# Moving the tables of the last 16 heads into an idle activation block, and giving the residuals two buffers and GpSimd's queue

## The chip, the cores and the metric

The kernel runs on one core of a Trainium2 chip. A core has a matrix engine (PE; its weight loads are shown apart as PEld), a vector engine (DVE), a scalar engine (ACT), GpSimd (POOL) and a sync engine (SP) that here only issues DMAs. Each engine works through its own instructions in order and waits on semaphores for the others. The metric is device time in microseconds (us) of one execution, the median of several. A second kind of number comes from one profiled execution: its span, the busy time of each engine and the waits between instructions.

## The reference

The input `x` is 32 sequences x 64 channels (heads) x 1024 positions. Each head gets a state space convolution, each sequence is masked to its length, and then the last axis of 1024 goes through a gated feed-forward layer whose weights are 4 bit (GPTQ). The residual is added at the end. Cut to what matters:

```python
# convolution, per head h: kernel of length 1024 from 64 complex modes
dtA = (-exp(log_A_real) + 1j * A_imag) * exp(log_dt)[:, None]
K = 2 * einsum('hn,hnl->hl', Cc * (exp(dtA) - 1) / A, exp(dtA[:, :, None] * arange(1024))).real
u = x * mask                                   # mask: position < length of the sequence
y = (causal_convolution(u, K) + u * D) * mask  # written with an FFT of length 2048
# feed-forward, 1024 -> 2752 -> 1024, weights w = (q - z - 1) * s, s per group of 128 rows
gate, up = y @ Wg, y @ Wu
inter = gate * sigmoid(gate) * up
out = x + (inter @ Wd).astype(float16)
```

## The kernel before

The 64 heads x 32 sequences are 2048 columns, in four blocks of 512 columns (16 heads each). Positions and hidden units lie on the 128 partitions.

**The convolution of a block.** The kernel values of 8 heads come from tables. `decays` (L475) makes exponentials, `tables` (L443, calling `phase_tables`, L183) makes sines and squares, `factors` (L460, calling `kernel_factors`, L213) combines them on DVE into `e1t` and `e2t`. `make_kernel` (L421) multiplies these on PE (L425, L427), splits the product into two halves of 16 bit (L430 on ACT, L431 on DVE) and writes them to a DRAM buffer `kpad` (L433). `toeplitz` (L514) loads for one head a 512 KB matrix `t` from `kpad`, each row one place further on (L525, SP's queue). There are three `t` buffers. `conv_load` (L500) loads the input `u` of four heads. `conv_head` (L531) does one head: eight steps of three small matmuls each (L548). After every second head DVE masks the sum into `y` (L560), ACT rounds it to 16 bit `xh` (L563), and POOL computes the remainder `xl` (L565). The pair `xh`, `xl` of a block is kept in an activation buffer. There are two of them, `x[0]` for blocks 0 and 2 and `x[1]` for blocks 1 and 3, each 128 x 8 x 512 twice.

**The feed-forward.** A chain is one PSUM tile (128 x 2 x 512) that is multiplied up over groups of 128 rows and scaled between the groups, because every group has its own scale. `gu_one` and `gu_pair` (L678) do gate and up, 8 groups per chain; `dn_pair` (L718) does the down product for 256 of the 1024 outputs, 21 groups and a remainder (L736, L737, L741). After each group the PSUM tile is rescaled in place, by DVE (L637, `rescale_two`) or by two ACT instructions (L640), and PE's next group of that chain waits for this. Three or four chains are in flight, so PE works on the others meanwhile. At the end of a `dn_pair` chain the sum is scaled into `o` (L754 on DVE or L758 on ACT), the residual `xr` (512 KB, `residual`, L772) is added by POOL for one half and by DVE for the other (L762), and two stores of 256 KB go out (L767). `o` and `xr` have two buffers each.

**Stages.** `roll` (L780) runs eight stages: 0 and 1 gate and up of the blocks 0 and 1 for four column tiles, 2 the rest of gate and up for both, 3 the four down chains of block 0, 4 those of block 1, 5 gate and up of blocks 2 and 3, 6 and 7 their down chains. Beside the chains it advances side generators, listed in `sides` (L1040) with a rate: so many steps of the generator for each step of a chain. With `None` as the last entry the generator is advanced only if the planner's own clock has room on DVE and ACT (`room`, L327), and dropped at the stage's end; with `True` it is run to its end when the stage ends, with nothing between its steps. The order in which instructions stand on each engine comes from this plan and from a scheduler beneath it that may move an instruction whose inputs are known ahead of others.

**Around the change.** In stages 3 and 4 the convolutions of blocks 2 and 3 run beside the down chains (`convs`, L1024, 1.9 steps for each chain step). Block 3 needs the kernels of heads 48 to 63, which `fourth` (L1003) makes in two groups of eight. `fourth` first waits until all down weights are unpacked, closes the pool of the unpacking (`up_stack`) and opens a pool `kg2` in its room. It uses `x[1]` as scratch for the phase tables and the decays, since `x[1]` is free from the end of stage 2 until block 3's first heads are written. `convs` runs block 2, then forces all of `fourth`, then runs block 3. The residuals of blocks 0 to 2 are loaded by SP's queue into buffers that they share with `sg`, the output of the gate's activation (tag `sg`, two buffers), and so stand between SP's loads of `t` and `u`.

Of the kernel before, what the change touches and what calls it, by code (L numbers as in the profile page):

```python
# [9 lines left out]
F32 = mybir.dt.float32  # L10
# [19 lines left out]
KSCALE = 64.0  # L30
PLACES = {("a", "pair"): 1, ("a", "single"): 2, ("b", "pair"): 3}
MAGIC = 12582912.0
RATES = {"first": (0.5, 4.6), "fill": (1.0, 0.8), "third": 0.5, "convs": 1.9}
HOP, MM, LANDING = 220.0, 215.7, 6000.0
LAG, HEAD_STARTS = 2, [4, 2, 1]
DVE_ROOM, ACT_ROOM = 1200.0, 1500.0
# [211 lines left out]
def every(gen):  # L248
    for _ in gen:
        pass  # L250
# [8 lines left out]
class Core:  # L259
    def __init__(self, ctx, tc, io):  # L260
        self.tc, self.nc, self.io = tc, tc.nc, io
        pool = lambda name, **k: ctx.enter_context(tc.tile_pool(name=name, **k))
# [11 lines left out]
        self.forced = True  # L274
        self.bank_free = {"a": [], "b": []}
        self.kpad = self.dram.tile([H, 2, 1152], F16, name="kpad")
        self.dm, self.known, self.ready = {}, set(), set()
        self.marks = {}
        self.sg, self.t0, self.us, self.raw = {}, {}, {}, {}
# [438 lines left out]
    def dn_pair(self, k, blk, place):  # L718
# [8 lines left out]
        for g in range(GI):  # L727
# [14 lines left out]
            if g < 21:  # L742
# [4 lines left out]
                    nc.scalar.dma_start(self.ihl[:, g], self.spill[g])  # L747
                    self.loaded[blk + 1, g] = True
                yield
        xr = self.res[k] if blk == 3 else self.residual(self.fw, 2 * k, blk)  # L750
        take = self.last_o if blk == 3 else lambda shape, dt: self.fw.tile(shape, dt, name="o", bufs=2)
        o = take([128, 2, 512], F16)
        if not apart and self.on_dve(1240, 1380):
# [17 lines left out]

    def residual(self, pool, n0, blk):  # L772
        rows, cols = slice(128 * n0, 128 * n0 + 256), slice(512 * blk, 512 * blk + 512)
        xr = pool([128, 2, 512], F32) if callable(pool) else pool.tile([128, 2, 512], F32, name="xr", tag="sg", bufs=2)
        self.nc.sync.dma_start(
            xr, self.io["xT"].rearrange("l h b -> l (h b)")[rows, cols].rearrange("(k p) t -> p k t", p=128))
        return xr

# [64 lines left out]
def tile_ssm_ffn(ctx, tc, io):  # L843
    nc = tc.nc
    c = Core(ctx, tc, io)
# [141 lines left out]
    third_it = third()  # L987
# [13 lines left out]
        return make  # L1001

    def fourth():  # L1003
        c.forced = True
        every(third_it)
        c.forced = False
        while not c.ready.issuperset(("dn", k, part) for k in range(4) for part in range(3)):
            yield
        c.up_stack.close()
        with tc.tile_pool(name="kg2", bufs=1, side="right") as kg2:  # L1010
            space = c.x[1]
            yield from c.decays(c.scratch(space[:1]), (48, 56))
            c.taps(kg2, 48)
            for h0 in (48, 56):
                yield from c.tables(ScratchPool(c.scratch(space[1:])), h0, 8)
                yield from c.factors(kg2, h0, 8, c.xds[h0])
                for _ in range(3):
                    yield
                c.make_kernel(kg2, h0, 8, "a")
                yield  # L1020

    fourth_it = fourth()

    def convs():  # L1024
        yield from c.conv(2)
        c.forced = True
        c.need(*(("dn", k, part) for k in range(4) for part in range(3)))
        every(fourth_it)
        c.forced = False
        yield from c.conv(3)  # L1030

    def residuals():
# [3 lines left out]
        yield  # L1036

    convs_it = convs()
    second_it = second()
    sides = {  # L1040
        0: [(unpack_it, RATES["first"][0], None), (group_it, 1.0, None), (second_it, RATES["first"][1], True)],
        1: [(unpack_it, RATES["fill"][0], None), (third_it, RATES["fill"][1], None)],
        2: [(third_it, RATES["third"], None), (unpack_it, RATES["fill"][0], None)],
        3: [(unpack_it, RATES["fill"][0], None), (fourth_it, RATES["fill"][1], None), (convs_it, RATES["convs"], False)],
        4: [(fourth_it, RATES["fill"][1], None), (convs_it, RATES["convs"], True)],
        6: [(residuals(), 1.0, True)],
# [80 lines left out]
```

## Time and profile before

| | |
|---|---|
| time, median of 3 runs | 1074.12 us (1073.29 to 1074.46) |
| the profiled execution's own time | 1075.33 us |
| its span, first to last instruction | 1073.5 us |
| PE busy | 1026.2 us, 96% |
| DVE busy | 803.7 us, 75% |
| ACT busy | 775.6 us, 72% |
| POOL busy | 246.5 us, 23% |
| mean granted PE clock | 0.992 |

The page of the profile gives busy time by engine, the span in 40 slices, the DMA queues, the chain of work that ended last, the costliest groups of instructions, and the DMAs with the time from issue to landing. Queries give the same for a stretch of time: busy time by engine and granted clock (stretches), the instructions in order (timeline), who waited for whom (waits). A matmul's shown time, 0.38 us for 512 columns, includes the length of the pipeline; back to back such matmuls start 0.2157 us apart, so a busy PE may still have lost a little at each restart. Times below are counted from the span's start. Stages 3 and 4 lie at about 404 to 585 us.

### The profile page before, as it was taken

To read this page: it belongs to the slowest core of one execution; us is meant where nothing else is said; L and a number is where in the kernel's file an instruction comes from. 1 tells how busy PE (TensorE), PEld (TensorE's weight loads), DVE (VectorE), ACT (ScalarE), POOL (GpSimd) and SP (SyncE) were. 2 spreads that over 40 slices of the span, in tenths; PEclk is the share of its full clock that TensorE was granted. 3 is DMA by queue.
4 is the path that set the end of the run, shared out by engine and by line. 5 is a ranking of instruction groups with operands and counts; after the bars stand their busy time and mean duration, and the time that the engine had idled before them with its cause. 6 is when DMAs were issued, how large, how long until landed. Compare 5 with 4: busy or idle time off the path is not lost.

```text
span 1073.5 us, 15382 instructions
## 1 busy us (share of the span) xinstructions
PE 1026.2 (96%) x5854; PEld 513.5 (48%) x5854; DVE 803.7 (75%) x939; ACT 775.6 (72%) x1034; POOL 246.5 (23%) x270
## 2 busy tenths in 40 slices
PE   3989999999999999997999999999999999999996
PEld 2867444444344445663665444444444444444442
DVE  8965788888977786768446777777877777777776
ACT  5767777787677777777577777666666667878775
POOL 0333233232332242231103112221111222102102
PEclk9999999999999999999999999999999999999998
DMA  6976321111111534546753001000000001424102
GB/s 197 331 244 211 101 69 40 40 59 40 42 48 50 143 88 156 164 156 196 231 167 128 30 29 51 20 13 17 20 20 20 20 20 58 129 79 148 59 1 79
DMA packets 52099, 99.76 MB, mean 93 GB/s; under 512 B 9524, under 2 KB 11444, under 8 KB 52024
## 3 DMA queue, kind: packets, MB, share of 16 engines
q1 hardware_dynamic: 38888, 70.09, 20.8%
q0 software_dynamic: 5280, 17.31, 4.3%
q10 hardware_dynamic: 7856, 11.37, 3.6%
q8 instruction: 46, 0.75, 0.3%
q14 instruction: 29, 0.24, 0.1%
HBM read 78.99 MB, written 19.76 MB: 92 GB/s over the span
## 4 chain that ended last, share of the span: by engine, by line
PE 83%; ACT 5%; DMA 4%; DVE 4%; issue 2%; POOL 0%; SPq 0%; DVEq 0%; ACTq 0%
PE chq L687 23%; PE chq L688 22%; PE chq L736 13%; PE chq L737 13%; PE cq L548 6%; PE chq L664 2%; PE chq L665 2%; DMA t<-kpad 2%; ACT chq L640 1%; DVE chq L618 1%; ACT chq L620 1%; DVE v L700 1%; DMA ihl<-kpad 1%; DMA ihl<-xF 1%; PE chq L741 1%
## 5 line engine op out<-in xcount | busy, mean ns | idle before, releaser
L687 PE MATMUL chq<-xh,w 128*128 128x512 f16 x1216 | 460.4, 380 | 5.7 <-DVE chq L618 2.1
L688 PE MATMUL chq<-xl,w 128*128 128x512 f16 x1216 | 458.6, 380 | 0.0
L618 DVE TENSOR_SCALAR chq<-chq,gur 128x1024 f32<-128x1024 f32 x261 | 333.2, 1289 | 95.3 <-PE chq L688 94.1
L620 ACT ACTIVATE chq<-chq,gur 128x1024 f32<-128x1024 f32 x285 | 304.3, 1085 | 86.8 <-PE chq L688 85.5
L640 ACT ACTIVATE chq<-chq,dnr 128x512 f32<-128x512 f32 x372 | 242.1, 661 | 71.7 <-PE chq L737 63.8
L736 PE MATMUL chq<-ihl,wd 128*128 128x512 f16 x672 | 253.8, 380 | 6.5 <-ACT chq L640 3.5
L737 PE MATMUL chq<-ihl,wd 128*128 128x512 f16 x672 | 253.4, 380 | 0.0
L637 DVE TENSOR_TENSOR chq<-chq,dnr 128x1024 f32<-128x1024 f32 x129 | 158.4, 1231 | 83.6 <-PE chq L737 83.2
L688 PEld LDWEIGHTS <-w 128*128 128x128 fp8e4 x1216 | 118.9, 98 | 155.3 <-issue 19.4
L687 PEld LDWEIGHTS <-w 128*128 128x128 fp8e4 x1216 | 118.9, 98 | 145.9 <-issue 1.9
L310 POOL TENSOR_TENSOR ihl<-v,ihl 128x512 f16<-128x512 f32 x42 | 48.3, 1150 | 362.9 <-ACT ihl L629 362.9
L737 PEld LDWEIGHTS <-wd 128*128 128x128 fp8e4 x672 | 65.5, 98 | 76.0 <-issue 12.7
L548 PEld LDWEIGHTS <-t 128*128 128x128 f16 x1152 | 81.4, 98 | 39.2 <-DMA t<-kpad 5.9
L736 PEld LDWEIGHTS <-wd 128*128 128x128 fp8e4 x672 | 65.7, 98 | 67.7 <-issue 1.7
L548 PE MATMUL cq<-uh,t 128*128 128x256 f16 (+3 forms) x720 | 91.8, 226 | 4.6 <-DMA t<-kpad 4.5
L565 POOL TENSOR_TENSOR xl<-y,xh 128x512 f16<-128x512 f32 x28 | 36.2, 1294 | 161.5 <-ACT xh L563 161.5
L548 PE MATMUL cq<-ul,t 128*128 128x256 f16 (+3 forms) x360 | 71.6, 225 | 0.0
L629 ACT CAST ihl<-v 128x512 f16<-128x512 f32 x42 | 25.9, 617 | 58.7 <-DVE v L700 55.3
L700 DVE SCALAR_TENSOR_TENSOR v<-chq,gul,sg 128x1024 f32<-128x1024 f32 x38 | 48.6, 1280 | 17.1 <-PE chq L688 11.3
L310 POOL TENSOR_TENSOR spill<-v,spill 128x512 f16<-128x512 f32 x42 | 48.8, 1161 | 14.2 <-ACT spill L629 13.9
L640 ACT ACTIVATE chq<-chq,gur 128x512 f32<-128x512 f32 x66 | 43.2, 661 | 11.0 <-PE chq L665 9.8
L590 POOL TENSOR_TENSOR w<-w,z 128x256 int32<-128x256 int32 x42 | 31.5, 770 | 82.0 <-DVE w L584 77.6
(250 smaller groups left out, 820.5 us busy)
## 6 DMA issues: line engine op xcount, KB each, us to landing
t<-kpad SPq DMA_DIRECT2D x48, 512.0 KB, 4.4
spill<-spill POOLq DMA_DIRECT2D x42, 256.0 KB, 2.7
ihl<-spill ACTq DMA_DIRECT2D x42, 256.0 KB, 2.8
z<-zc SPq DMA_DIRECT2D x29, 256.0 KB, 3.7
u<-xF SPq DMA_DIRECT2D x12, 512.0 KB, 3.7
xr<-xT SPq DMA_DIRECT2D x12, 512.0 KB, 4.7
out<-xr POOLq DMA_DIRECT2D x24, 256.0 KB, 2.9
w<-qgu SPq DMA_DIRECT2D x21, 256.0 KB, 4.1
```

Source lines behind the costliest of these rows:

```text
L310: self.nc.gpsimd.tensor_tensor(out, a, b, op)
L548: nc.tensor.matmul(q[:, d:, h % 2, :], t0[:, lw, 128 * d:128 * d + 128], uu[:, 0:8 - d, h % 4, :], start=(d == 0 and k == 0 and h % 2 == 0 ...
L565: split.tensor_tensor(xl[:, :, ts], yv, xh[:, :, ts], ALU.subtract)
L618: self.mark("dve", self.nc.vector.tensor_scalar(q, q, col, None, ALU.mult))
L620: self.mark("act", self.nc.scalar.activation(q, q, AF.Copy, scale=col))
L637: self.mark("dve", self.nc.vector.tensor_tensor(q, q, cols.to_broadcast([128, 2, 512]), ALU.mult))
L640: self.mark("act", self.nc.scalar.activation(q[:, k], q[:, k], AF.Copy, scale=cols[:, k]))
L687: nc.tensor.matmul(q[:, b], lw, xh[:, g, :], start=(g == 0), stop=False, skip_group_check=True)
L688: nc.tensor.matmul(q[:, b], lw, xl[:, g, :], start=False, stop=(g == GH - 1), skip_group_check=True)
L700: nc.vector.scalar_tensor_tensor(v, q, last, self.sg.pop(ct - 21), ALU.mult, ALU.mult)
L736: nc.tensor.matmul(qs[j], lw, self.ihl[:, g, 0], start=(g == 0), stop=False, skip_group_check=True)
L737: nc.tensor.matmul(qs[j], lw, self.ihl[:, g, 1], start=False, stop=False, skip_group_check=True)
```

## The change

Three things change.

The residuals of blocks 0 to 2 no longer share buffers with `sg`. At the end of the first down chain the kernel makes sure that all down weights are unpacked, closes the pool of the unpacking, and opens a pool `xrp` of two buffers in its room. These residuals are loaded by GpSimd's queue, which also carries their stores. The residuals of block 3 stay with SP.

`fourth` takes all its room from `x[1]`: decays, the D coefficients, phase tables, factors and the split kernel. It waits neither for the unpacking nor for the third group of tables, so its steps can begin with stage 3. The three fixed pauses before `make_kernel` become a wait on the planner's clock.

`convs` doesn't force `fourth` after block 2; it idles until heads 56 to 63 are known, and forces only at the stage's end. Its rate goes from 1.9 to 1.52 steps for each chain step.

```diff
-RATES = {"first": (0.5, 4.6), "fill": (1.0, 0.8), "third": 0.5, "convs": 1.9}
+RATES = {"first": (0.5, 4.6), "fill": (1.0, 0.8), "third": 0.5, "convs": 1.52}
...
+        self.xrp = None
...
-        xr = self.res[k] if blk == 3 else self.residual(self.fw, 2 * k, blk)
+        if blk == 3:
+            xr = self.res[k]
+        else:
+            if self.xrp is None:
+                self.need(*(("dn", j, part) for j in range(4) for part in range(3)))
+                self.up_stack.close()
+                self.xrp = self.up_stack.enter_context(self.tc.tile_pool(name="xrp", bufs=2, side="right"))
+            xr = self.residual(self.xrp, 2 * k, blk)
...
-        xr = pool([128, 2, 512], F32) if callable(pool) else pool.tile([128, 2, 512], F32, name="xr", tag="sg", bufs=2)
-        self.nc.sync.dma_start(
+        xr = pool([128, 2, 512], F32) if callable(pool) else pool.tile([128, 2, 512], F32, name="xr")
+        (self.nc.sync if callable(pool) else self.nc.gpsimd).dma_start(
...
     def fourth():
-        c.forced = True
-        every(third_it)
-        c.forced = False
-        while not c.ready.issuperset(("dn", k, part) for k in range(4) for part in range(3)):
+        first, second = c.x[1]
+        yield from c.decays(c.scratch([first[:, :4]]), (48, 56))
+        c.taps(ScratchPool(c.scratch([first[:, 4:6]])), 48)
+        for h0 in (48, 56):
+            small = ScratchPool(c.scratch([first[:, 6:8], second[:, 7:8]]))
+            yield from c.tables(ScratchPool(c.scratch([second[:, :7]])), h0, 8)
+            yield from c.factors(small, h0, 8, c.xds[h0])
+            yield from c.pause(c.td - c.tp + HOP)
+            c.make_kernel(small, h0, 8, "a")
             yield
-        c.up_stack.close()
-        with tc.tile_pool(name="kg2", bufs=1, side="right") as kg2:
-            space = c.x[1]
-            yield from c.decays(c.scratch(space[:1]), (48, 56))
-            c.taps(kg2, 48)
-            for h0 in (48, 56):
-                yield from c.tables(ScratchPool(c.scratch(space[1:])), h0, 8)
-                yield from c.factors(kg2, h0, 8, c.xds[h0])
-                for _ in range(3):
-                    yield
-                c.make_kernel(kg2, h0, 8, "a")
-                yield
...
     def convs():
         yield from c.conv(2)
-        c.forced = True
-        c.need(*(("dn", k, part) for k in range(4) for part in range(3)))
-        every(fourth_it)
-        c.forced = False
+        while 56 not in c.known:
+            if c.forced:
+                next(fourth_it)
+            yield
         yield from c.conv(3)
```

## The prediction

> **What bounds the kernel now.** I read the page first, for the engines' shares, then the busy time by stretch over stages 3 and 4, then the chain and the timeline inside the bad stretch, then the table of DMAs. The page and the three stretches:
>
> ```profile
> PE 1026.2 (96%) x5854; PEld 513.5 (48%) x5854; DVE 803.7 (75%) x939; ACT 775.6 (72%) x1034; POOL 246.5 (23%) x270
> ```
>
> ```profile
> 404.00:486.00 82.00, 81.71 (x644) 49.27 (x642) 55.97 (x66) 61.66 (x94) 26.33 (x31) 1.00 0.50 162
> 486.00:520.00 34.00, 26.14 (x199) 13.98 (x196) 22.50 (x39) 20.38 (x37) 2.72 (x4) 0.95 0.68 216
> 520.00:585.00 65.00, 65.00 (x511) 39.03 (x510) 35.23 (x33) 49.52 (x78) 14.44 (x15) 1.00 0.54 171
> 250.00:300.00 50.00, 47.11 (x207) 20.22 (x206) 42.78 (x48) 36.88 (x41) 16.53 (x18) 0.97 0.15 48
> ```
>
> The columns after the stretch are PE, PEld, DVE, ACT, POOL busy, the granted clock, the DMA share and GB/s. PE is the bound nearly everywhere, so only PE's own idle time can be won. Of stages 3 and 4, 486 to 520 stands out: 26.14 of 34 us busy at a clock of 0.95. The stretches on both sides lose 0.3 us in 147. The chain and the timeline say what happens there:
>
> ```profile
> 491.24 1.24 ACT chq L640 x2
> 492.50 1.28 ACT L207
> 493.79 0.94 ACT xl L207 x2
> 494.73 0.82 ACT xl L209 x2
> ...
> 504.58 5.92 DMA t<-kpad
> 510.55 1.71 PE cq L548 x24
> 512.27 4.72 DMA t<-kpad
> ```
>
> ```profile
> 495.18 0.38 PE L736 MATMUL chq<-ihl,wd 128*128 128x512 f16 x1 [2.21 <-DVE chq L637]
> ```
>
> The forced `fourth` puts a table load, sines, squares and some twenty DVE operations in one lump between the rescales, so down chains wait (2.21 us at 495.18). Then PE waits for `t` of head 48, which needs the kernel just written, and again for the fourth `t`. How much is lost: the rows of that stretch hold 67 down matmuls x 0.2157 = 14.5 us, 96 convolution matmuls (four heads at 1.5, from the start of head 48 to that of head 49 in the timeline) = 6.0, four L425 at 0.28 and 32 L427 at 0.039 (both from the chain) = 2.4. That is 22.9 us of work in 34: **11.1 us lost**.
>
> **The change part by part.** The built order of the changed program shows where things go. Up to the start of stage 3, and on PE from the end of block 3's convolution on, the order is the old one, so all differences lie in about 404 to 585 us and in the waits for residuals.
>
> *Removed: the lump.* Group 48's `make_kernel` now stands 77 us of PE work after the start of stage 3, group 56's at 105 us, and head 48's convolution begins right after the latter. Its `t` depends on group 48 alone, known 30 us earlier, so the 5.92 us wait goes. SP also loses the residual loads, one of which waited 7 us for a store among the `t` and `u` loads. Gain: 11.1 us at most; all of it, as neither the lump nor the load behind it is left. Moved but not removed: one exponential and one sine table load (1.28 each), the exponential (1.06), eight sines and squares (0.62 or 0.40): 8.4 us on ACT; on DVE, per group, 14 operations of 0.34 to 0.74, together 7.0, so 13.9 for both. 22.3 us on two engines. Both stay below PE in the sum: of 181 us, DVE is busy 113.7 and ACT 131.6.
>
> *Added 1: these operations between the rescales of stages 3 and 4.* A chain has its turn on PE about every 3.4 us (three chains of 0.86 plus convolution). Its rescale takes 1.23 on DVE or 1.36 on ACT, so about 1 us of delay is hidden; one place holds 3.3 us of DVE work between two rescales, another a table load and a sine between the halves of one ACT rescale. Lower bound: 0, since the unpacking (DVE operations of 0.5 to 0.8 us in pairs) ran in 404 to 486 with 0.3 us lost. Upper bound: stage 2 has the same two groups for heads 32 to 47, there with DVE 86% busy; 250 to 300 lost 2.9 us of idle time and 1.5 of clock, 4.4; with the fuller queues at the three chain ends I allow 6. A gain below zero is excluded, as the work only comes on top of the rescales. I take 2.5, nearer to the unpacking because DVE here is 68% busy, not 86%.
>
> *Added 2: a drain.* At 1.52 steps instead of 1.9, and with steps spent idling until group 56 is known, block 3 isn't through when the last down chain has been begun. The order shows 192 convolution matmuls, heads 56 to 63, back to back with no down matmul among them, where before there were 18. Alone they need 8 x 1.5 = 12 us of PE, which is no new work. But three `t` buffers don't keep up. Let L be the time from the end of a head to the start of the head that takes over its buffer. Head 55 ends about 0.9 us before the drain, heads 56 and 57 are loaded. Heads 59 and 60 start at 1.5 + L and 3 + L, 62 at 3 + 2L, 63 right after it, and the drain ends at 6 + 2L. Its loss is 2L - 6. The trace has one clean L: head 48 ended at 512.2, its buffer's next head began at 517.04, L = 4.84, loss 3.7. Lower bound: the fastest `t` loads land in 3.6, L = 4.0, loss 2.0. Upper bound in the ordinary case: 5.3 as landing (one at 531.5), L = 5.65, loss 5.3. I take 3.7. During the drain 512 KB per 1.9 us are moved, and the stores and two residuals beside it; the page's fullest slice has 331 GB/s, so this is near the limit, and why the upper end is kept.
>
> *Added 3: residuals on POOL.* The DMAs that matter, with KB each and the median us from issue to landing:
>
> ```profile
> t<-kpad SPq DMA_DIRECT2D x48, 512.0 KB, 4.4
> spill<-spill POOLq DMA_DIRECT2D x42, 256.0 KB, 2.7
> ihl<-spill ACTq DMA_DIRECT2D x42, 256.0 KB, 2.8
> xr<-xT SPq DMA_DIRECT2D x12, 512.0 KB, 4.7
> out<-xr POOLq DMA_DIRECT2D x24, 256.0 KB, 2.9
> ```
>
> POOL spends 0.55 us on issuing 256 KB, so 1.1 on a residual: 12 x 1.1 = 13 us on an engine that is 23% busy, hidden. A load that waits for two stores to land holds POOL for up to 4 us; behind it stand `xl` (L565), which frees one of two `y` buffers, and adds. In stages 3 and 4 the next `y` that needs the buffer comes 10 us later, in the drain 5 us or more: hidden, and if not, a bank of the convolution waits. In stage 5 POOL is idle for 10 us at a time: zero. DVE's half of the add waits for the load with rescales behind it. For the third chain of stage 3 it may wait 1 us, with table operations behind it: nothing. In stage 6 the third residual is asked for when the first one's stores have landed (984.7), landed at 989.4, and DVE added it at 989.74 with 0.6 us lost by PE. From POOL it comes 0 to 1 us later. I take 0.4. The `sg` buffers, freed of residuals, gain nothing: stage 5 loses 0.1 us in 315.
>
> One rule speaks against this part. The rows first: POOL's 256 KB stores land in 2.9, ACT's loads of that size in 2.8, though DVE is 75% busy. The Trainium skill, "SBUF — State Buffer", section "SBUF: two separate sides", says that a DMA issued by GpSimd can be held up while DVE runs an operation that takes both its ports; its figures are 620 ns alone and 3100 beside one. By the rule, as an estimate, the third residual of stage 6 would come 2.5 us later instead of 0.4, and the sum would be 2.1 us worse.
>
> *Clock.* The slow clock at 497 (0.72 in 495 to 500, 0.94 in the next 5 us) cost 1.7 us and is in the 11.1. It followed PE gaps of at most 2.4 us. The drain's gaps are about as long, so it may come again: price 1.7, not in the sum. The Trainium skill, "TensorE: Matmul & The Clock Gate", section "What's actually happening", asks for a whole idle window of about 3.4 us; by that the drain would never slow down, but neither would this place have.
>
> *Sum.* -11.1 + 2.5 + 3.7 + 0.4 = -4.5 us. The profiled execution took 1075.33 (span 1073.5 and 1.8 around it) and would take 1070.8. It lies 1.2 above the median of 1074.12, so as a median: **1069.6 us**.
>
> **The rivals.**
>
> *A. The new work breaks the down chains (slower).* Place: DVE and ACT in stages 3 and 4. If half of the 22.3 us shows on PE, 11.2: -11.1 + 11.2 + 3.7 + 0.4 = +4.2, 1078.3. For: the lump did just this at 492 to 505, and ACT is 73% busy. Against: paced by the planner's room, as the unpacking is. It decides from 9.2 us on (9.2 + 4.1 - 11.1 = 2.2).
>
> *B. The drain eats the gain (no change).* Three `t` loads issued together at 504.6 landed after 5.9, 6.9 and 8.2. With L = 7 the drain loses 8; with a slow clock, 1.7: -11.1 + 2.5 + 9.7 + 0.4 = +1.5, 1075.6. Against: that batch shared the queues with `u` and `ihl` loads, and in the drain at most two are young at once.
>
> *C. All hidden (faster still).* Tables 0.3, drain 2.0, residuals 0: -8.8, 1065.3.
>
> *D. POOL's waits for stores hold `y` and with it the convolution's bank (slower).* 4 us in the drain twice: -11.1 + 2.5 + 3.7 + 8 = +3.1, 1077.2. Against: the 5 us above.
>
> That the change doesn't do what it says is excluded by the order: the tables do stand early, the loads do stand on POOL. But the rate leaves the drain behind.
>
> **How the numbers follow.** A measurement tells 0.2%, 2.15 us: faster is below 1071.97, slower above 1076.27. Likeliest case 0.50, C 0.20, B 0.17, A 0.10, D 0.03. So faster 0.70, same 0.17, slower 0.13. The bounds of the likeliest case alone: -11.1 + 0 + 2.0 + 0 = -9.1 to -11.1 + 6 + 5.3 + 1 = +1.2, so 1065.0 to 1075.3. The range for 8 in 10 reaches from C to just short of B: 1065.0 to 1075.3 as well; A, D and the worst of B are left out.
>
> **What would show it.** Right: 486 to 520 like its neighbours, no wait of PE for DVE or ACT over 1 us in stages 3 and 4, and then a stretch of about 16 us near its end with DVE and ACT nearly idle and PE waiting for `t` three or four times, 0.5 to 2.5 us each, DMA share near 0.9. The third residual add of stage 6 shows a DVE wait for a DMA on POOL's queue. Wrong: PE gaps of 1 us and more spread over stage 3 with a table operation or a table load as releaser (A), a drain of 20 us (B), `y` waiting for POOL (D), or a slow clock in the drain.

## The result and the profile after

The changed kernel takes **1082.74 us** (median of 4 runs, 1082.33 to 1084.19), the kernel before 1073.9 us in the same comparison (4 runs). The ratio is 1.0076, 95% interval 1.0063 to 1.0089: slower by 0.76%. The forecast was 1069.6 us in a range to 1075.3. In a later group the changed kernel, run again, stood at 1.0061 (1.0044 to 1.0078). The profiled execution took 1082.75 us, with a span of 1081.0 and 1.8 around it, 7.5 us more span than before.

Line numbers from here on are those of the changed kernel: L549 convolution matmuls, L737, L738 and L742 down matmuls, L638 (DVE) and L641 (ACT) rescales, L192 to L209 table operations, L770 the additions of the residuals, L775 their stores, L783 their loads, L591 POOL's part of the unpacking.

The engines' line of the page, after:

```profile
PE 1027.8 (95%) x5854; PEld 514.4 (48%) x5854; DVE 814.2 (75%) x943; ACT 769.6 (71%) x1026; POOL 254.9 (24%) x282
```

PE's work is the same. DVE has 10.5 us more busy time: the planner gave it five more rescales of the down chains (134 in place of 129, 6.2 us; ACT has 6.0 us less) and one scaling of `o` less (1.2), and the rest comes from operations that took longer (last section). From here on stages 3 and 4 are counted from their first down matmul, at 395.5 us before and 395.0 after, not from 404. Busy time by stretch, after (PE, PEld, DVE, ACT, POOL, clock, DMA share, GB/s):

```profile
400.00:480.00 80.00, 78.13 (x565) 44.13 (x564) 61.97 (x78) 62.51 (x98) 22.58 (x27) 1.00 0.42 132
480.00:510.00 30.00, 25.01 (x167) 14.05 (x164) 22.40 (x24) 14.30 (x24) 8.98 (x11) 0.89 0.74 251
510.00:568.00 58.00, 57.87 (x424) 32.72 (x423) 33.53 (x35) 44.27 (x70) 7.86 (x8) 1.00 0.55 172
568.00:587.00 19.00, 13.44 (x197) 12.40 (x195) 5.94 (x7) 5.32 (x9) 9.97 (x12) 1.00 0.83 277
```

The lump of before at 486 to 520 is gone as such: 510 to 568 loses next to nothing. But a hole stands at 480 to 510, where PE is idle 5 us and the clock is 0.89, and another in the drain, 568 to 587, where PE is idle 5.6 us.

**The first hole.** PE's waits from 470 to 520 us, after:

```profile
PE chq L737 <- DVE chq L638: 4.8, 2, 4.1
```

PE waits 4.1 us at once for a rescale by DVE (L638). DVE's timeline says what DVE was doing (start, us, instruction, and in brackets its idle time and what ended it):

```profile
476.83 0.69 DVE L770 TENSOR_TENSOR xr<-xr,o 128x512 f32<-128x512 f32 x1 [1.68 <-DMA xr<-xT]
...
488.32 1.64 DVE L770 TENSOR_TENSOR xr<-xr,o 128x512 f32<-128x512 f32 x1 [2.89 <-DMA xr<-xT]
489.88 0.68 DVE L200 SCALAR_TENSOR_TENSOR xl<-xl 128x512 f32<-128x512 f32 x1
490.48 0.41 DVE L201 SCALAR_TENSOR_TENSOR xl<-xl 128x256 f32<-128x256 f32 x1
490.82 1.22 DVE L638 TENSOR_TENSOR chq<-chq,dnr 128x1024 f32<-128x1024 f32 x1
```

It waited 2.89 us for the third residual. Behind the addition stood two table operations, and behind them the rescale that PE needed. POOL's timeline shows why the residual was late:

```profile
470.82 1.44 POOL L591 TENSOR_TENSOR wd<-wd,z 128x256 int32<-128x256 int32 x2 [1.14 <-DVE wd L585]
472.56 1.47 POOL L783 DMA_DIRECT2D xr<-xT  x2 [0.30 <-POOL wd L591]
476.90 1.64 POOL L770 TENSOR_TENSOR xr<-xr,o 128x512 f32<-128x512 f32 x1 [2.87 <-DMA xr<-xT]
478.83 1.13 POOL L775 DMA_DIRECT2D out<-xr  x2 [0.30 <-POOL xr L770]
483.36 0.72 POOL L783 DMA_DIRECT2D xr<-xT  x1 [3.40 <-DMA out<-xr]
```

The two buffers lie in the unpacking's room, so the first two loads can't be issued before the last unpacking, at 472.56. The addition follows at 476.90, the stores at 478.83, and the third load has to wait until the first residual's stores have landed, 483.36. It lands 4.8 us later. Before, the third load was issued at 480.86 and landed at 484.65, just as the chain's sum `o` was ready. DVE added it without a wait, and the next rescales followed at once (L762 is the addition there, L637 the rescale):

```profile
484.77 0.69 DVE L762 TENSOR_TENSOR xr<-xr,o 128x512 f32<-128x512 f32 x1
485.38 2.36 DVE L637 TENSOR_TENSOR chq<-chq,dnr 128x1024 f32<-128x1024 f32 x2
```

**The drain.** The chain of work from the first convolution after the last down matmul:

```profile
568.01 3.06 PE cq L549 x48
571.09 6.88 DMA t<-kpad
578.02 1.71 PE cq L549 x24
579.74 4.97 DMA t<-kpad
584.75 1.69 PE cq L549 x24
```

and the DMAs of 564 to 586 us (KB each, median us from issue to landing):

```profile
t<-kpad SPq DMA_DIRECT2D x6, 512.0 KB, 6.7
out<-xr POOLq DMA_DIRECT2D x4, 256.0 KB, 6.2
xr<-xT POOLq DMA_DIRECT2D x2, 512.0 KB, 5.9
```

The loads of `t`, 4.4 us over the whole run before, take 6.7 here, beside POOL's stores and residuals. At 575 to 580 the DMA share is 1.04 at 381 GB/s. All three kinds of DMA land later than their medians over the whole run, which are 4.8, 3.7 and 4.4 after.

**The end.** From the start of the last matmul to the end of the span it is 10.47 us, 9.48 before. The difference lies in GpSimd's closing instruction, a drain of its queue: 8.24 us in the trace after, 7.26 before.

To size these I use one measure for all kernels. For each matmul, the time to the next matmul's start, less what a matmul of its kind takes back to back (the lower quartile of all of its kind), is time that PE lost, to a wait or to a slow clock. In 400 to 590 us it adds up to 14.2 before and 20.8 after:

| us lost by PE | 400 to 480 | 480 to 510 | 510 to 560 | 560 to 590 |
|---|---|---|---|---|
| before | 1.6 | 10.5 | 1.5 | 0.6 |
| after | 4.3 | 8.6 | 0.9 | 7.0 |

Of the 8.6 us at 480 to 510, some 3.3 are the slow clock (30 us at 0.89), which comes right behind PE's gap; the gap itself is 4.3. Stages 3 and 4, from the first down matmul to the first of stage 5 behind the convolutions, last 184.65 us before and 191.33 after.

### The profile page after: what moved, and what is told of

The parts are those of the page before. It is cut to its first block, busy times and chain, and to the rows that moved or that the text cites. A ratio compares the mean times of both kernels' runs of the same rounds, so it can differ in the third digit from the quotient of the medians.

```text
span 1081.0 us, 15379 instructions
## 1 busy us (share of the span) xinstructions
PE 1027.8 (95%) x5854; PEld 514.4 (48%) x5854; DVE 814.2 (75%) x943; ACT 769.6 (71%) x1026; POOL 254.9 (24%) x282
## 4 chain that ended last, share of the span: by engine, by line
PE 72%; issue 8%; DVE 7%; ACT 6%; DMA 5%; POOL 2%; DVEq 0%; POOLq 0%; ACTq 0%
PE chq L688 23%; PE chq L689 22%; PE chq L737 9%; PE chq L738 9%; PE cq L549 4%; PE chq L665 2%; PE chq L666 2%; ACT chq L641 2%; DMA t<-kpad 2%; DMA xr<-xT 1%; DVE v L701 1%; DVE chq L619 1%; ACT chq L621 1%; DMA out<-xr 1%; DMA ihl<-kpad 1%
## 5 line engine op out<-in xcount | busy, mean ns | idle before, releaser
L641 ACT ACTIVATE chq<-chq,dnr 128x512 f32<-128x512 f32 x362 | 235.4, 661 | 75.9 <-PE chq L738 69.1
L737 PE MATMUL chq<-ihl,wd 128*128 128x512 f16 x672 | 253.9, 381 | 7.4 <-DVE chq L638 4.8
L738 PE MATMUL chq<-ihl,wd 128*128 128x512 f16 x672 | 253.3, 381 | 0.0
L638 DVE TENSOR_TENSOR chq<-chq,dnr 128x1024 f32<-128x1024 f32 x134 | 163.8, 1231 | 74.7 <-PE chq L738 72.1
L738 PEld LDWEIGHTS <-wd 128*128 128x128 fp8e4 x672 | 65.9, 98 | 78.7 <-issue 13.3
L549 PEld LDWEIGHTS <-t 128*128 128x128 f16 x1152 | 81.1, 98 | 39.8 <-DMA t<-kpad 8.7
L737 PEld LDWEIGHTS <-wd 128*128 128x128 fp8e4 x672 | 65.6, 98 | 69.9 <-DVE wd L600 1.6
L549 PE MATMUL cq<-uh,t 128*128 128x256 f16 (+3 forms) x720 | 90.4, 227 | 8.3 <-DMA t<-kpad 8.1
L549 PE MATMUL cq<-ul,t 128*128 128x256 f16 (+3 forms) x360 | 71.5, 226 | 0.0
L641 ACT ACTIVATE chq<-chq,gur 128x512 f32<-128x512 f32 x66 | 43.2, 661 | 11.0 <-PE chq L666 9.8
L591 POOL TENSOR_TENSOR w<-w,z 128x256 int32<-128x256 int32 x42 | 31.6, 772 | 81.2 <-DVE w L585 77.6
```

Of the source, the lines that this page charges most:

```text
L549: nc.tensor.matmul(q[:, d:, h % 2, :], t0[:, lw, 128 * d:128 * d + 128], uu[:, 0:8 - d, h % 4, :], start=(d == 0 and k == 0 and h % 2 == 0 ...
L638: self.mark("dve", self.nc.vector.tensor_tensor(q, q, cols.to_broadcast([128, 2, 512]), ALU.mult))
L641: self.mark("act", self.nc.scalar.activation(q[:, k], q[:, k], AF.Copy, scale=cols[:, k]))
L737: nc.tensor.matmul(qs[j], lw, self.ihl[:, g, 0], start=(g == 0), stop=False, skip_group_check=True)
L738: nc.tensor.matmul(qs[j], lw, self.ihl[:, g, 1], start=False, stop=False, skip_group_check=True)
```

## The experiments

Three theories at first. **Buffers**: the late room and the two buffers make DVE wait for the third residual. **Queue**: it is GpSimd's queue that makes the loads late. **Tables**: the table operations between the rescales break the chains. The drain comes beside each of them. All edits are against the changed kernel. The sixteen kernels ran in four groups of four (e1 to e4, e5 to e8, e9 to e12, e13 to e16), each on another chip and beside the kernel before, which in the second group spread from 1072.65 to 1081.49 us over 31 runs. So ratios are compared, with some care between groups, and with them the losses in the profile, which are those of a single execution.

| kernel | ratio, 95% interval | stages 3 and 4 | lost 400 to 480 | lost 480 to 510 | drain: matmuls, us lost |
|---|---|---|---|---|---|
| after | 1.0076 (1.0063 to 1.0089) | 191.33 | 4.3 | 8.6 | 192, 6.4 |
| e1_own_sp | 1.0055 (1.0039 to 1.0071) | 192.82 | 4.3 | 4.9 | other order |
| e2_sg_pool | 1.0038 (1.0023 to 1.0053) | 188.69 | 4.6 | 5.4 | 207, 7.0 |
| e3_sg_sp | 1.0041 (1.0026 to 1.0055) | 191.22 | 4.6 | 9.6 | 207, 5.3 |
| e4_rate21 | 1.0014 (0.9998 to 1.0029) | 186.65 | 2.1 | 10.9 | 81, 1.2 |
| e5_four_buffers | 1.0029 (1.0015 to 1.0042) | 188.64 | 4.3 | 4.4 | 192, 8.1 |
| e6_adds_pool | 1.0048 (1.0031 to 1.0064) | 188.65 | 4.3 | 4.9 | 192, 7.8 |
| e7_four_rate21 | 1.0025 (1.0011 to 1.0039) | 185.17 | 2.0 | 9.3 | 81, 1.3 |
| e8_four_adds_rate20 | 0.9953 (0.9937 to 0.9969) | 178.25 | 2.2 | 3.9 | 78, 0.5 |
| e9_t0_four | 1.0037 (1.0025 to 1.0049) | 189.23 | 4.3 | 7.7 | 192, 5.3 |
| e10_four_adds | 1.0046 (1.0031 to 1.0061) | 188.59 | 4.3 | 3.7 | 192, 8.9 |
| e11_adds_rate20 | 0.9957 (0.9944 to 0.9969) | 177.95 | 2.2 | 3.3 | 78, 0.8 |
| e12_all | 0.9944 (0.9932 to 0.9955) | 177.20 | 2.1 | 3.5 | 78, -0.1 |
| e13_after | 1.0061 (1.0044 to 1.0078) | 192.56 | 4.8 | 9.9 | 192, 6.3 |
| e14_no_residuals | 0.9936 (0.9922 to 0.9951) | 180.74 | 4.4 | 1.4 | 192, 3.1 |
| e15_rate20 | 0.9966 (0.9954 to 0.9979) | 178.95 | 2.2 | 3.9 | 78, 0.8 |
| e16_adds_rate20_sp | 0.9931 (0.9919 to 0.9944) | 179.02 | 2.2 | 4.5 | 78, 0.7 |

### Queue and buffers, taken back one at a time

Own buffers, but SP's queue for the loads:

```diff
-        (self.nc.sync if callable(pool) else self.nc.gpsimd).dma_start(
+        self.nc.sync.dma_start(
```

> The changed kernel, but the residuals of blocks 0 to 2 are loaded by SP's queue again, still into the two buffers of their own. Theory 1, buffers: PE's 4.5 us gap at 487.6 comes from the room of these buffers, which is free only when the unpacking has ended (first load at 473.3 instead of 400.7), and from the third load, which must wait for the stores out of the first buffer; then the gap stays, DVE again waits 2 us or more for the third residual, and the time stays within 2.5 us of 1082.7. Theory 2, queue: the gap comes from GpSimd's queue, where the loads wait in order behind other work; then DVE waits less than 0.5 us and the time falls by about 6, to 1076 to 1077.5. Theory 3, tables: neither matters, the late tables among the rescales make the gap; 1082 to 1083.

Measured: 1080.25 us. DVE still waits 2.17 us for the third residual. The planner's order came out otherwise: the last convolutions stand in runs of 96, 72 and 24 matmuls, and SP, which waits 30.1 us in all for stores to land with loads of `t` behind it, lets PE wait 4.5 us for a `t` at 577. At 480 to 510 PE still waits 3.3 us at once for DVE; what is gone is the slow clock behind it (1.00 there). The queue alone isn't the cause.

The buffers of `sg` again, but POOL's queue:

```diff
-            if self.xrp is None:
...
-            xr = self.residual(self.xrp, 2 * k, blk)
+            xr = self.residual(self.fw, 2 * k, blk)
...
-        xr = pool([128, 2, 512], F32) if callable(pool) else pool.tile([128, 2, 512], F32, name="xr")
+        xr = pool([128, 2, 512], F32) if callable(pool) else pool.tile([128, 2, 512], F32, name="xr", tag="sg", bufs=2)
```

> The changed kernel, but the residuals share the two buffers of sg again, as before; GpSimd's queue still loads them. Theory 1, buffers: the first two loads go out near 400, the gap of 4.5 us and the slow clock after it vanish, 1075.5 to 1077.5. Theory 2, queue: the gap stays, 1081 to 1084. Theory 3, tables: the gap stays, 1081 to 1084. The drain at the end of stage 4 has 207 convolution matmuls instead of 192, which costs 0.5 more on all theories.

Measured: 1078.97 us, between the theories. Here the first load isn't late, yet DVE waits 4.62 us for the third, and PE 2.4 us for the rescale behind it. And with both edits, the residuals wholly as they were before:

> The changed kernel with the residuals wholly as before (buffers of sg, SP's queue): what remains is the placing of the late tables and the rate. Theories 1 and 2: no gap at 487, 1075 to 1077.5, so above the kernel before only by the drain (6.5 lost) less what is left of the lump. Theory 3, tables: 1081 to 1084.

Measured: 1079.74 us, again between the theories. DVE waits 1.62 us for the third residual, so the late room isn't needed for that wait. But the 9.6 us that PE loses at 480 to 510 come from elsewhere. What PE waited for in e3_sg_sp, and SP's timeline:

```profile
PE cq L549 <- DMA t<-kpad: 4.0, 1, 4.0
PE chq L737 <- DMA ihl<-spill: 2.1, 1, 2.1
```

```profile
493.60 0.39 SPq L779 DMA_DIRECT2D xr<-xT  x1
494.08 2.42 SPq L526 DMA_DIRECT2D t<-kpad  x2
```

PE waits for no rescale of DVE there. A residual load (L779) stood on SP's queue until stores had landed (8.9 us for the longest such wait), with loads of `t` behind it, and a slow clock followed PE's 4.0 us wait (0.50 at 500 to 505). This is a cost that the move to GpSimd's queue was to remove.

What all four combinations share is that a third load waits for the first residual's stores, on whichever queue, and that DVE waits for this load. In three of them PE waits behind it for a rescale (4.1, 3.3 and 2.4 us). That these residuals were in time before rested on the old order of the work.

### The drain shortened

```diff
-RATES = {..., "convs": 1.52}
+RATES = {..., "convs": 2.1}
```

> The changed kernel with the convolution's rate at 2.1 instead of 1.52. The longest run of convolution matmuls without a down matmul at the end of stage 4 falls from 192 to 81. If the drain's 6.5 us come from t loads that three buffers can't hide, about 4 to 5 of them go: 1077.5 to 1079.5, and the gap near 487 stays. If they come from the stores and residuals that share the DMA engines with it, less than 2 go: 1081 to 1083.

Measured: 1076.29 us. The drain shrinks to 81 matmuls and loses 1.2 us, and 400 to 480 loses 2.1 in place of 4.3. But the hole at 480 to 510 grows to 10.9, of which some 3.3 are the slow clock (0.89), as in the changed kernel. DVE's timeline of e4_rate21:

```profile
476.95 1.23 DVE L638 TENSOR_TENSOR chq<-chq,dnr 128x1024 f32<-128x1024 f32 x1 [0.51 <-PE chq L738]
480.32 0.69 DVE L770 TENSOR_TENSOR xr<-xr,o 128x512 f32<-128x512 f32 x1 [2.13 <-DMA xr<-xT]
480.93 1.64 DVE L194 TENSOR_TENSOR xl<-wl,cst 128x512 f32<-128x512 f32 x1
...
484.09 0.74 DVE L203 SCALAR_TENSOR_TENSOR xl<-xl,cst 128x512 f32<-128x512 f32 x1
```

and ACT's, of the same kernel:

```profile
484.86 0.63 ACT L207 ACTIVATE xl<-xl 128x512 f32<-128x512 f32 x1 [3.47 <-DVE xl L203]
485.40 1.22 ACT L641 ACTIVATE chq<-chq,dnr 128x512 f32<-128x512 f32 x2
```

Now it is the first residual that is late. Behind its addition stand the table operations L194 to L203, behind L203 an ACT table operation, and behind that the rescale for which PE starts no matmul from 482.62 to 486.09. One late load went through two engines.

### Four buffers, and the additions taken from DVE

```diff
-    ... tile_pool(name="xrp", bufs=2, side="right"))
+    ... tile_pool(name="xrp", bufs=4, side="right"))
```

> The changed kernel with four residual buffers instead of two, everything else as changed. No load then waits for a store of stage 3. Theory 1, two buffers: in all four runs so far DVE waited 1.6 to 4.6 us for the third residual, whose load had waited for the first one's stores, with either queue and either pair of buffers; with four that wait is below 0.5, PE's gap of 4.3 us near 488 and the slow clock of 1.7 us after it go, and the kernel is 4 to 6 us faster than the changed one: 1.002 to 1.004 of the kernel before. Theory 3, tables: the gap comes from table operations in DVE's queue; it stays above 3 us and the ratio stays above 1.006. The drain is untouched by both: 192 matmuls, 6 to 7 us lost.

Measured: 1079.03 us. The third load no longer waits for a store, DVE no longer waits for the third residual, and the slow clock behind PE's gap doesn't come (1.00): the loss at 480 to 510 falls from 8.6 to 4.4. (DVE still waits 1.7 us for the first.) The drain then loses 8.1 instead of 6.4.

```diff
-            (nc.vector if j == 1 else nc.gpsimd).tensor_tensor(xr[:, j], xr[:, j], o[:, j], ALU.add)
+            (nc.vector if j == 1 and blk == 3 else nc.gpsimd).tensor_tensor(xr[:, j], xr[:, j], o[:, j], ALU.add)
```

> The changed kernel with two buffers, but GpSimd adds both halves of the residuals of blocks 0 to 2, so that DVE never waits for a residual. The third residual comes as late as in the changed kernel. Theory 1: what hurts is that DVE stands in line behind a late residual; PE's gap near 488 falls below 1.5 us and the ratio to 1.002 to 1.005. Theory 3, tables: no change, above 1.006. If the late residual itself holds the chains, by the buffers of o, the gap stays too, but then DVE's o waits for GpSimd's add.

Measured: 1080.45 us; 480 to 510 loses 4.9, the drain 7.8. DVE never waits for a residual, though the two buffers stay. Both edits at the old rate, run in a later group:

> The changed kernel with four residual buffers and both residual additions of the first three blocks on GpSimd, at the rate of 1.52. If each of the two alone already takes the whole gap behind the third residual away, both together are worth no more than one: stages 3 and 4 last 188.6 us again (a drain of 192 matmuls that loses 7 to 8 us), 1078 to 1080 us. If what each leaves is the other's, the gains add: 186 us, about 1076 us.

Measured: 1080.34 us. As expected if each takes the same thing away: stages 3 and 4 last 188.59 us, and 188.64 and 188.65 with one of the edits. Between 3.7 and 4.9 us are won at 480 to 510 in the three, of which 3.3 are the slow clock, and some 2 us are lost again in the drain, which now also meets a slow clock (0.50 to 0.57 at 576 to 582) that in the changed kernel had come at 489 to 498.

What is left at 480 to 510 has other causes. One is DVE operations that take longer beside POOL's, with a rescale that PE waits for behind them (L204 with 2.97 us in place of 0.47 in e5_four_buffers, L201 with 2.83 in e6_adds_pool; last section). Another is what PE waited for in e10_four_adds:

```profile
PE chq L737 <- DMA ihl<-spill: 2.5, 2, 1.8
```

PE waits for the loads of `ihl` on ACT's queue, 1.1 us in e5_four_buffers, 2.2 in e6_adds_pool and 2.5 here. Those for which it waits in e10_four_adds landed after 7.5 and 8.2 us, 2.6 over the whole run after, with a DMA share of 1.0 at 480 to 490. The run without residuals (below) has no such wait, so this too looks like a price of the residuals, by way of the DMA engines; no run tells it apart.

### Both parts together

Four buffers and rate 2.1; then four buffers, the additions on POOL and rate 2.0:

> Four residual buffers and a convolution rate of 2.1 together: both suspected costs are taken away, and the late tables stay in the idle activation block. If the two are all that ate the gain, the excess of 14 us that the kernel before has in stages 3 and 4 falls to 5 to 7 (tables 2.5, rest of the drain 2, ordinary 1.5) and the ratio to 0.992 to 0.995, faster than both kernels. If the tables themselves cost more than 5 us, 0.998 to 1.002.

> Four buffers, both adds on GpSimd and a rate of 2.0 (longest run of convolution matmuls 78). DVE is relieved of 24 half adds less 4. If DVE's wait for residuals is gone with four buffers already, the same as the run with four buffers and 2.1, within 0.2%; if loads that come late still hold DVE there, 1 to 2 us faster.

Measured: 1078.26 and 1070.33 us. The first is slower than the kernel before (1.0025), where 0.992 to 0.995 was expected. It still has the hole of e4_rate21 (DVE waits 1.83 us for the first residual, then the same table operations), as four buffers don't bring the first load forward. The second beats both kernels. Which of its three parts does it? With two buffers:

> Two residual buffers as in the changed kernel, both residual additions of the first three blocks on GpSimd, rate 2.0 (a drain of 78 matmuls). If VectorE's standing in line for the residual was the cost and not the number of buffers, the third load may be as late as in the changed kernel and nobody but GpSimd waits: stages 3 and 4 last 178 to 180 us and the time is 1069 to 1072 us. If the four buffers are needed, the first or third residual holds the rescales or the tables and it is 1074 to 1077 us.

Measured: 1070.81 us, so four buffers aren't needed.

### The loads of `t`, and a version with all parts

```diff
-            t0 = self.cv.tile([128, 2, L], F16, name="t0", bufs=3)
+            t0 = self.cv.tile([128, 2, L], F16, name="t0", bufs=4)
...
-        for k in range(hh, hh + (16 if hh < 16 else 6 if hh < 32 else 3)):
+        for k in range(hh, hh + (16 if hh < 16 else 6 if hh < 32 else 4)):
```

(`third` asks for the same number of buffers.)

> The changed kernel with four buffers for the tables t of the convolutions, and loads asked for four heads ahead in place of three. The residuals stay as in the changed kernel, so the gap at 487 to 492 us stays in both theories. If the drain of 192 convolution matmuls loses its 6.5 us because three loads in flight are too few for a landing of about 7 us, four give one late load of L - 3 x 1.5 = 2.2 us in place of two: 4 us less, about 1078.5 us. If the drain is held by what the DMA engines can move beside GpSimd's stores and residuals (busy share 0.9 to 1.04 there), the loads only wait longer: landings of 8 to 9 us, a loss of 5 us or more, 1081 to 1083 us.

Measured: 1079.46 us, between the theories. The waits for `t` in the drain fall from four (1.4, 2.7, 1.3 and 0.8 us of lost time) to two (0.7 and 2.7), as the first theory has it, but the loads land after 8.1 us instead of 6.7, as the theory of full DMA engines has it. A slow clock behind that wait (0.50 at 579 to 582) takes part of the gain; the drain loses 5.3 in place of 6.4.

With this, three residual buffers, the additions on POOL and rate 2.0:

> Three residual buffers, both additions of the first three blocks on GpSimd, rate 2.0, and four buffers for the tables t with loads four heads ahead. If the drain of 78 matmuls loses 0.5 us only, as it did at this rate, a fourth buffer has at most that to give: 1069.5 to 1070.5 us. If the convolutions among the down matmuls wait for their loads too, up to 2 us more: 1068 us.

Measured: 1069.05 us. The drain loses nothing any more.

### What remained open: whose fault is each hole?

The changed kernel itself in the same group:

> The changed kernel itself, beside the three other runs of this group, so that they stand against it on one chip: a ratio of 1.0076 to the kernel before, as measured first; stages 3 and 4 of 191 us, 8.6 us lost at 480 to 510 and 6.4 us in the drain.

Measured: 1082.02 us. DVE waited 4.9 us for the third residual this time, PE 5.3 us for DVE.

Without the residuals of the first three blocks:

```diff
-            xr = self.residual(self.xrp, 2 * k, blk)
...
         for j in range(2):
+            if blk < 3:
+                break
             n = 2 * k + j
```

> The changed kernel without the residuals of the first three blocks: their loads, additions and stores are left out, so three quarters of the output is not written. The order on TensorE and the rate of 1.52 stay. If the drain loads are late because they share the DMA engines with the residuals and stores of GpSimd's queue, the drain of 192 matmuls now has a landing of 4 to 5 us and loses 2 to 3.7 us; if the loads of t by themselves fill the engines, it still loses 6 us or more. If the third residual makes the loss at 480 to 510 us, 8.6 us become 3 us or less there; if the table operations do, 7 us or more stay. First theory of both: stages 3 and 4 last 181 to 184 us, 1071 to 1074 us. Rival of both: 189 to 191 us, 1079 us or more.

Measured: 1068.04 us. Stretches of e14_no_residuals, in the columns above:

```profile
480.00:510.00 30.00, 29.23 (x230) 17.16 (x230) 22.70 (x29) 19.56 (x33) 2.31 (x2) 1.00 0.56 182
510.00:564.00 54.00, 53.87 (x395) 30.60 (x394) 29.03 (x28) 41.07 (x65) 3.47 (x3) 1.00 0.51 157
564.00:580.00 16.00, 13.60 (x198) 12.52 (x196) 3.92 (x6) 5.33 (x9) 4.62 (x4) 1.00 0.61 198
```

and the loads of its drain:

```profile
t<-kpad SPq DMA_DIRECT2D x5, 512.0 KB, 4.4
```

The residuals are behind most of the first hole and about half of what the drain loses. The same table operations and the same 192 matmuls are there, but 480 to 510 loses 1.4 us instead of 8.6 and the drain 3.1 instead of 6.4, and `t` lands after 4.4 us. The tables theory falls as the cause of the hole: without the residuals the new order costs 4.4 - 1.6 = 2.8 us at 400 to 480 and at most these 1.4 behind. And the 2.8 aren't the tables' alone. The longest wait of PE there, 0.8 us, is for an unpacked weight (L600), and at rates of 2.0 and 2.1 the same operations run and the stretch loses 2.0 to 2.2 us, 0.4 to 0.6 more than before. (The time also holds a shorter end, 7.52 us, of which more below.)

The rate alone:

> The changed kernel at a rate of 2.0, with the order on TensorE of the runs that were faster than before (a drain of 78 matmuls). VectorE still adds half of each residual. If the drain is the larger part by itself, its 6 us go and nothing else changes: 185 us in stages 3 and 4, about 1076 us. If VectorE's wait for the residual keeps costing at the higher rate, 480 to 510 us loses 9 to 11 us and it is 1075 to 1077 us, against 1071 with the additions on GpSimd: then the two parts don't add, and 5 us or more of the price of the residuals is hidden behind the drain. If the wait costs nothing at this rate, 1071 us.

Measured: 1071.61 us, the last of the three cases: at 2.0 the stretch 480 to 510 loses 3.9 us, while at 2.1 it lost 10.9. DVE's timeline of e15_rate20:

```profile
477.94 1.98 DVE L600 TENSOR_SCALAR wd<-wd 128x1024 fp8e4<-128x1024 uint8 x2
479.84 0.68 DVE L770 TENSOR_TENSOR xr<-xr,o 128x512 f32<-128x512 f32 x1
480.45 1.22 DVE L638 TENSOR_TENSOR chq<-chq,dnr 128x1024 f32<-128x1024 f32 x1
...
492.08 0.69 DVE L770 TENSOR_TENSOR xr<-xr,o 128x512 f32<-128x512 f32 x1 [1.51 <-DMA xr<-xT]
492.69 1.23 DVE L638 TENSOR_TENSOR chq<-chq,dnr 128x1024 f32<-128x1024 f32 x1
```

At 2.0 the first residual is there when two operations of the unpacking are done, and a rescale, not the table operations, stands next. The third residual is asked for later than in the changed kernel and is waited for 1.51 us, with a rescale right behind it. So the residual's price is set by what stands in line around the addition, and a rate of 0.1 more moves that. So of the three parts of e8_four_adds_rate20 it is the rate that counts. The additions on POOL matter little at it: they give 0.9957, half of them on DVE 0.9966, and the intervals overlap (other group).

At last SP's queue in that version (the edits of e1_own_sp, e6_adds_pool and rate 2.0):

> Two residual buffers, both additions on GpSimd, rate 2.0, and SyncE's queue for the loads of the residuals in place of GpSimd's. GpSimd's closing drain took 8.24 us in the changed kernel and 7.26 before, and the time from the last matmul to the end was 10.47 us in all runs with the loads on GpSimd's queue and 9.48 with them on SyncE's: if this comes from the loads on GpSimd's queue, it is 9.48 us here, and the time is 1 us below the run with GpSimd's queue, about 1069.8 us. If the loads, waiting for stores, hold the loads of t behind them on SyncE's queue, up to 5 us come on top: 1074 us.

Measured: **1068.36 us**, 0.9931 of before, the lowest ratio of the kernels that compute everything, though its interval overlaps that of e12_all. From the last matmul to the end it takes 9.49 us, as expected. SP waited for stores without making a `t` late (1.4 us lost at 560 to 590). The 1.0 us at the end isn't all of the difference to e11_adds_rate20 (0.9957, another group): in the profiled executions its stages 3 and 4 are 1.1 us longer than there, so where the rest of the ratio comes from stays open.

## Why the prediction was wrong

Its sum was -11.1 + 2.5 + 3.7 + 0.4 = -4.5 us. Step by step, in us lost by PE:

| step | predicted | measured |
|---|---|---|
| Removed: the lump | -11.1 | -11.1 (480 to 560 lost 12.0 before; 510 to 560 loses 0.9) |
| Added 1: tables among the rescales | +2.5 (0 to 6) | +2.7 at 400 to 480, and at most 1.4 behind |
| Added 2: drain | +3.7 (2.0 to 5.3) | +6.4; 3.1 with no residuals beside it |
| Added 3: residuals on POOL | +0.4 | 7.2 of the 8.6 at 480 to 510, 3.3 in the drain, 1.0 at the end |

(The 7.2 and 3.3 are the changed kernel less the run without residuals; that run also lacks stores that the kernel before had.) The rows add to -11.1 + 2.7 + 1.4 + 3.1 + 7.2 + 3.3 = +6.6 in stages 3 and 4, where 6.7 was measured, and 1.0 at the end; the span grew by 7.5.

**Added 3 failed.** The sentence was: "For the third chain of stage 3 it may wait 1 us, with table operations behind it: nothing." DVE waited 2.89 us, and the rescale that PE needed stood behind those very table operations. The prediction looked at what stood directly behind the addition and not at what stood behind that. It didn't follow the chain of the two buffers either, load, addition, stores landing, next load, from the moment at which their room comes free. With the times of the changed trace, 472.56 + 4.2 to land, 1.65 for the addition, 3.6 for the stores and 4.8 for the next load put the third residual at 486.8 or later, behind the 484.65 of before. The first of these numbers couldn't be read from the old trace: there POOL's last unpacking ended at 465.7, in the changed kernel at 472.3.

Two things qualify the row. Its name says too much: with queue and buffers as before (e3_sg_sp) stages 3 and 4 last 191.22 us, 0.1 less, so what cost the 7.2 isn't the move to POOL as such but residuals that meet another order of the work. There the old queue had its own price, a late `t`. And of the 7.2 some 3.3 are the slow clock, which the prediction priced at 1.7 and left out of its sum.

**Added 2 was mis-sized**, with the right mechanism. The formula 2L - 6 and L = 4.84 fit the run without residuals (3.1 lost, 15.12 us long, 15.7 predicted). With the residuals `t` landed after 5.0 to 8.2 us. The signs came as written: PE waited for `t` four times, for 0.8 to 2.7 us. The prediction named the drain "near the limit" of what the DMAs can move, but took L from one load with no transfer of POOL's queue beside it, and left rival B's L = 7 because that batch "shared the queues". In the drain it shared the DMA engines with POOL's transfers. By the formula the 6.4 us lost are an L of 6.2, above the 5.65 of the prediction's upper bound and below B's 7.

**Removed came out as predicted, and Added 1 near it**, the latter partly by luck: DVE was slower than assumed (below), and a good part of the 2.7 goes with the rate (2.0 and 2.1 lose 0.4 to 0.6). The slow clock, outside the sum, did come again: 0.50 at 492 to 498, behind the PE gap at 487.56, not in the drain where it was expected.

Of the rivals, B saw the drain, and D's wait is in the trace: DVE waited 6.36 us for `xl` in the drain, but PE was waiting for `t` then. Its price was nothing, as argued. Stage 6 cost nothing of note, DVE waiting 0.8 us for one residual there. No rival had a late residual in stage 3.

## What to carry to other kernels

A buffer's next load waits for its last store, so follow a residual through load, addition, store and load again, and then read two places further down the line of the engine that adds: if the work that the bottleneck needs stands there, give the addition to an engine with nothing urgent behind it (here 0.3% at most at the rate of 1.52, nothing clear at 2.0). A stretch that runs on loads alone is priced with the landing times of its own traffic, all queues together, not with those of a quiet moment. After a change that moves work, a rate that paces it is worth another look: 2.0 in place of 1.52 was worth 1.0% here (1.0061 to 0.9966 in one group), and 2.1 only 0.6% (1.0076 to 1.0014, two groups).

## What the runs showed of the hardware

**DVE stands still beside POOL.** DVE's timeline of e6_adds_pool:

```profile
481.73 0.69 DVE L200 SCALAR_TENSOR_TENSOR xl<-xl 128x512 f32<-128x512 f32 x1
482.33 2.83 DVE L201 SCALAR_TENSOR_TENSOR xl<-xl 128x256 f32<-128x256 f32 x1
```

and POOL's:

```profile
482.60 2.27 POOL L770 TENSOR_TENSOR xr<-xr,o 128x512 f32<-128x512 f32 x2
```

An operation that takes 0.41 us took 2.83 and ended 0.3 us behind POOL's two additions. Over 395 to 590 us, DVE operations beside a POOL addition or subtraction of f32 took 6.3 us longer in the changed kernel than the median of the same operations without one, against 0.9 before. Those that read PSUM (`chq`, `cq`) were not slowed (rescale 1.23 us either way). The Trainium skill, "SBUF — State Buffer", section "SBUF: two separate sides", says that DVE and GpSimd share a pair of ports that one of them holds for a whole instruction, on DVE's side in a mode with two ports or with two inputs from SBUF. The trace agrees so far: L201 has both inputs in SBUF. But by its recorded start L201 was 0.27 us ahead of the additions, and the page gives the ports to whichever starts first; there the row doesn't fit. Both kernels give POOL the same additions in these stages, so the 6.3 against 0.9 is a matter of what DVE does beside them: table operations, which work from SBUF, or rescales, which work in PSUM. The same section warns that a DMA of GpSimd's queue starves beside DVE, and the medians show no sign of that: residuals landed after 4.4 us from POOL's queue and 4.7 from SP's (medians of the page).

**GpSimd's queue has a price at the end of the kernel, for each DMA.** GpSimd's closing drain took 5.30 us with 42 DMAs on its queue (e14_no_residuals), 7.26 with 66 (before) and 8.24 with 78 (after): 0.082 us for each, in both steps. The twelve loads thus cost 1.0 us at the end, and in e16_adds_rate20_sp, with 66 DMAs, it took 7.25 again.

**The slow clock moves.** Gaps are counted here from the start of one matmul to the start of the next. In the kernel before, one of 2.6 us, with others of 1.3 and 0.9 near it, was followed by a clock of 0.57 in a 3 us slice; after, one of 4.5 by 0.50. In e1_own_sp one of 3.6 at 487 to 490 was followed by no slow clock, and one of 4.9 at 573 to 577 by 0.61. No single length of gap tells them apart here.
